# A third Winograd step for P4 in two products of a dense layer on Trainium2

## Chip, cores and metric

The kernel runs on one core of one Trainium2 chip. The metric is the device time of one execution in microseconds (us); lower is better. All data are fp32.

## What is computed

Two layers follow each other on x of 8 sequences, 256 tokens, 1024 channels. The first adds to x a dense product with W and a low-rank (LoRA) term whose experts are chosen for each token; the second adds a product with one of 16 matrices, chosen for each sequence.

```python
base = jnp.einsum('btd,od->bto', x, W)
logits = jnp.einsum('btd,ed->bte', x, Wr) + bias        # bias: 5.0 at the sequence's own expert
topw, topi = jax.lax.top_k(logits, 2)
weights = jax.nn.softmax(topw, axis=-1)
gates = jnp.sum(jax.nn.one_hot(topi, 8) * weights[..., None], axis=-2)
h = jnp.einsum('btd,erd->bter', x, A)                   # 8 experts of rank 16
x = x + base + 2.0 * jnp.einsum('bter,bte,eor->bto', h, gates, B)
x = x + jnp.einsum('bsi,boi->bso', x, L1_weight[adapter_ids])
```

Only layer one's dense product (`x + base`, and B of the LoRA term) is touched by the change.

## The kernel before, in words

**Layer one** is a matrix product in Winograd's form of Strassen's method: seven products in place of eight, and sums and differences of blocks around them. The outer step cuts W and x into 2 x 2 blocks each (`wb`, `xb`; a block of W is 512 x 512, one of x 512 channels by 1024 tokens) and makes seven products, with the keys "1" to "7" (`opening` makes key "1", `product` the others; they run in the order 1, 5, 2, 6, 3, 7, 4, lines 760 to 816). The residual is an identity added to W's diagonal blocks. Results are gathered in `yb`, four blocks of 128 x 4096, each seen as four quarters `dest[:, q]` of 128 x 1024.

**The second step** is inside each product: `make_subs` (L366) gives views `a(i, j)`, `b(i, j)` of quarters of the two factors, and their sums s1 to s3 and t1 to t3. `product` (L504) then runs seven inner products on TensorE (PE): a00 b00 into A, s1 t1 into B, s2 t2 into A, a01 b10 into X (a copy of A, made by ScalarE at L522), s3 t3 into A, **P3**, that is s2 b11, into B, and **P4**, that is a11 t2, into A. A, B and X are pairs of PSUM banks (128 x 2 x 512). Each inner product is four matmul calls (`mm`, L442 to L453): two chunks k of 128 channels, two halves m of 128 outputs, 512 tokens. The s2 and t2 that P3 and P4 read are remade by `late[0]` and `late[1]` (L562, L566). Where `lora` is given, `mm` adds the up projection, two more calls on B's rows and the gated `hg` (L443, L444).

**The third step** is in the products with `further` set (keys 5, 2, 3, 4): there a01 b10 goes down once more, as seven small products of one chunk, 128 outputs and 256 tokens (`deep`, L512). Their factors are differences r1 to r4 (128 x 128) and q1 to q4 (128 x 256), made by VectorE from `make_subs` (L390 to L403) into pool `sub3`, one buffer for each of the tags r13, r2, r4, q13, q2, q4. Two of PSUM's single banks, A3 and B3, gather what belongs to several quarters, and the rest goes into X itself. VectorE adds A3 (L551, L561, L576) and B3 (L577) into `dest[:, 0]`, and then X (L578).

**Who does what, in which order.** Each engine runs its instructions in the order in which the program issues them (`manual_schedule`, L752); the framework adds the waits. VectorE (DVE) does all sums and differences, and adds each accumulator into its quarter: `evict` (L431) is an addition on DVE where a base is given, and a copy on ScalarE where none is. All DVE additions are recorded under one line, L217. In between stands `pump(place)` (L335): it takes pieces of work off the list `todo` (block differences, the s, t, r, q of a later product, in pieces with an estimated time and an earliest place) and issues a share of what is left over the places 1 to 7. A pumped piece stands in DVE's queue ahead of what is issued after it.

In products 2 and 4 the base and the destination are y21 to y11 and y21 to y21 (L797, L816). During product 2, `todo` holds differences of x22, x12, w11 and w22 and the s and t of key 6; during product 4 it holds `prep_w1(0, 0)` and `prep_y(0)`, the adapter's first preparations.

**PSUM pairs rotate.** `roles` (L105) gives the next product the pair of the last one's X as A, that of B as X, and that of A as B. So the B of the product behind 2 (key 6, not `further`, which begins with four calls into A and then wants B) and that behind 4 (`adapt(0)`, the adapter of the first sequence, L648, likewise) stand on the pair that P4 was gathered in, and wait until DVE has read it. The single banks are also used by the transposes of `turn` and the last adapter.

**Layer two** (`adapt`, L648) is one Winograd step for each of the eight sequences, with the weights loaded by the SP queue (`load_w1`, L603) into the space of blocks that are read no more.

The end of `product`, where P3 and P4 stand:

```python
add(dest[:, 0], X, dest[:, 0])
pump(4)
mm(A, t["s3"], t["t3"])
add(dest[:, 3], A, dest[:, 3])
pump(5)
mm(B, t["s2"], b(1, 1), False, "d", 1)
add(dest[:, 1], B, dest[:, 1])
pump(6)
mm(A, a(1, 1), t["t2"], False, "1", 0)
evict(dest[:, 2], A, old[2])
pump(7)
```

Of the kernel before, what the change touches and what calls it, by code (L numbers as in the profile page):

```python
# [9 lines left out]
F32 = mybir.dt.float32  # L10
# [6 lines left out]
P = 128  # L17
# [8 lines left out]
def kernel(  # L26
# [320 lines left out]
    def us(n):  # L347
        return (n + 151) / 960
# [13 lines left out]
        return pieces(fn, wb[out_], wb[x], wb[y], 2)  # L362

    subs = {}

    def make_subs(key, w, x, further=True):  # L366

        def a(i, j):  # L370
            return wb[w][:, 2 * j : 2 * j + 2, i * OQ : (i + 1) * OQ]

        def b(i, j):
            return xb[x][:, 2 * i : 2 * i + 2, j * TQ : (j + 1) * TQ]


        ra = lambda i, j: a(0, 1)[:, j, ts(i, P)]
        rb = lambda i, j: b(1, 0)[:, i, ts(j, TQ // 2)]
        t = {}

        def op3(name, tag, fn, x, y, first=4):
            width = P if name[0] == "r" else TQ // 2

            def run():
                t[name] = sub3.tile([P, width], F32, name=f"{name}_{key}", tag=tag)
                fn(t[name], *(t[v] if isinstance(v, str) else v for v in (x, y)))

            return us(width), first, run

        deep = [  # L390
            op3("r1", "r13", add, ra(1, 0), ra(1, 1)),
            op3("q1", "q13", minus, rb(0, 1), rb(0, 0)),
            op3("r2", "r2", minus, "r1", ra(0, 0)),
            op3("q2", "q2", minus, rb(1, 1), "q1"),
            op3("r4", "r4", minus, ra(0, 1), "r2"),
            op3("q4", "q4", minus, rb(1, 0), "q2"),
        ]

        def deep3():
            for o in (  # L400
                op3("r3", "r13", minus, ra(0, 0), ra(1, 0)),
                op3("q3", "q13", minus, rb(1, 1), rb(0, 1)),
            ):  # L403
                o[2]()

        def op(name, fn, x, y, first):
            pool = sub2 if name[1] == "2" else sub1
            width = OQ if name[0] == "s" else TQ

            def run():  # L410
                t[name] = pool.tile([P, 2, width], F32, name=f"{name}_{key}", tag=name)
                fn(t[name], *(t[v] if isinstance(v, str) else v for v in (x, y)))

            return us(2 * width), first, run

        def late_s():
            minus(t["s2"], a(0, 1), t["s2"])

        def late_t():
            minus(t["t2"], b(1, 0), t["t2"])  # L420

        subs[key] = (a, b, t, (late_s, late_t), (ra, rb, deep3), further)
        return [
            op("s1", add, a(1, 0), a(1, 1), 3),
            op("t1", minus, b(0, 1), b(0, 0), 3),
            op("s2", minus, "s1", a(0, 0), 3),
            op("t2", minus, b(1, 1), "t1", 3),
            op("s3", minus, a(0, 0), a(1, 0), 5),
            op("t3", minus, b(1, 1), b(0, 1), 5),
        ] + (deep if further else [])  # L430

    def evict(dest, acc, base=None):

# [24 lines left out]
    def opening(key, dest):  # L458


        idle = pair("idle", 2)
        for i in range(WARM):
            nc.tensor.matmul(idle[:, 0, :P], lhsT=ident, rhs=ident, start=True, stop=True)  # L463
        mm = multiply()
        sums_of = make_subs(key, "11", "11", False)
        a, b, t, late, _, _ = subs.pop(key)
        X = pair(f"X_{key}", 0)
        A = pair(f"A_{key}", 1)
        add_identity(wb["11"], 0, 2)
        mm(X, a(0, 1), b(1, 0), True, part=(0,))  # L470
        project(0, 0, singles("ps_h_0_0"), (2,), last=False)
        mm(X, a(0, 1), b(1, 0), part=(1,))
        evict(dest[:, 0], X)
        project(0, 0, None, (3,), False, False)
        mm(A, a(0, 0), b(0, 0), True, part=(0,))
        project(0, 0, None, (0,), False, False)
        mm(A, a(0, 0), b(0, 0), part=(1,))
        project(0, 0, None, (1,), False, False)
        use_adapter_ids()
        add_identity(wb["11"], 2, 4)  # L480
        for s in sums_of[:4]:
            s[2]()
        add(dest[:, 0], A, dest[:, 0])
        nc.tensor.matmul(idle[:, 1, :NB], lhsT=ones, rhs=ids_f[:, :NB], start=True, stop=True)
        use_ids(idle[:, 1, :NB])
        B = pair(f"B_{key}", 2)
        mm(B, t["s1"], t["t1"], True)
        evict(dest[:, 3], B)
        for s in sums_of[4:]:
            s[2]()  # L490
        mm(A, t["s2"], t["t2"])
        evict(dest[:, 1], A)
        project(0, 0, None, range(KH, KC), False)
        take(0, 0)
        for f in late:
            f()
        mm(A, t["s3"], t["t3"])
        add(dest[:, 3], A, dest[:, 3])
        mm(B, t["s2"], b(1, 1))
        add(dest[:, 1], B, dest[:, 1])  # L500
        mm(A, a(1, 1), t["t2"])
        evict(dest[:, 2], A)

    def product(key, base, dest, lora=None, tokens=None):  # L504

        a, b, t, late, (ra, rb, deep3), further = subs.pop(key)
        mm = multiply(dict(zip("01d", b_part(lora))) if lora is not None else None, tokens)
        new = roles(key)
        old = [base[:, q] if base is not None else None for q in range(4)]
        n0, n1 = (slice(j * (TQ // 2), (j + 1) * (TQ // 2)) for j in range(2))  # L510

        def deep(acc, lhs, rhs, first=False):  # L512
            nc.tensor.matmul(acc, lhsT=lhs, rhs=rhs, start=first, stop=True, skip_group_check=True)  # L513

        def quarter(m, n):

            return dest[:, 0][:, m, n], old[0][:, m, n] if base is not None else None

        A = new("A")
        mm(A, a(0, 0), b(0, 0), True)  # L520
        X = new("X")
        nc.scalar.copy(X, A)  # L522
        if not further:
            pump(1)
            B = new("B")
            mm(B, t["s1"], t["t1"], True, "1", 1)
            evict(dest[:, 3], B, old[3])
            pump(3)
            mm(A, t["s2"], t["t2"])
            evict(dest[:, 1], A, old[1])  # L530
            pump(3)
            mm(X, a(0, 1), b(1, 0), False, "0", 0)
            late[0]()
            late[1]()
            evict(dest[:, 0], X, old[0])
# [8 lines that stand above are left out]
            evict(dest[:, 2], A, old[2])  # L544
            pump(7)
            return
        A3 = single(f"A3_{key}", 0)[:, n0]
        deep(A3, ra(0, 0), rb(0, 0), True)
        q, o = quarter(0, n0)
        evict(q, A3, o)  # L550
        pump(1)  # L551
        B = new("B")
        mm(B, t["s1"], t["t1"], True, "1", 1, ms=(0,))
        B3 = single(f"B3_{key}", 1)[:, n0]
        deep(B3, t["r1"], t["q1"], True)
        deep3()
        mm(A, t["s2"], t["t2"])
        evict(dest[:, 1], A, old[1])
        deep(A3, t["r2"], t["q2"])
        q, o = quarter(0, n1)  # L560
        evict(q, A3, o)  # L561
        late[0]()  # L562
        pump(2)
        mm(B, t["s1"], t["t1"], True, "1", 1, ms=(1,))
        evict(dest[:, 3], B, old[3])
        late[1]()  # L566
        pump(3)
        deep(X[:, 0, n0], ra(0, 1), rb(1, 0))
        deep(X[:, 0, n1], t["r4"], rb(1, 1))
        deep(X[:, 1, n0], ra(1, 1), t["q4"])  # L570
        mm(X, None, None, False, "0", 0, part=())
        deep(A3, t["r3"], t["q3"])
        two = [P, 2, TQ // 2]
        d1 = dest[:, 0][:, 1, :].rearrange("p (j n) -> p j n", j=2)
        both = A3.unsqueeze(1).to_broadcast(two)
        evict(d1, both, old[0][:, 1, :].rearrange("p (j n) -> p j n", j=2) if base is not None else None)  # L576
        add(dest[:, 0][:, :, n1], B3.unsqueeze(1).to_broadcast(two), dest[:, 0][:, :, n1])  # L577
        add(dest[:, 0], X, dest[:, 0])  # L578
        pump(4)
        mm(A, t["s3"], t["t3"])  # L580
        add(dest[:, 3], A, dest[:, 3])
        pump(5)
        mm(B, t["s2"], b(1, 1), False, "d", 1)
        add(dest[:, 1], B, dest[:, 1])
        pump(6)
        mm(A, a(1, 1), t["t2"], False, "1", 0)
        evict(dest[:, 2], A, old[2])
        pump(7)
# [285 lines left out]
```

## Time and profile before

| what | value |
|---|---|
| median of three runs | 428.77 us (428.74 to 429.66) |
| the profiled execution's own time | 430.16 us |
| its span, first to last instruction | 428.4 us |
| mean granted clock of TensorE | 0.999 |
| TensorE busy | 423.1 us (99%) |
| VectorE busy | 281.7 us (66%) |
| ScalarE busy | 39.6 us (9%) |
| DMA | 55.83 MB, 130 GB/s over the span |
| product 2 on TensorE | 92.98 to 123.47 us of the span |
| product 4 on TensorE | 202.03 to 232.52 us of the span |

All times in a view are counted from the start of the span. PE stands for TensorE's matmuls, PEld for its weight loads, DVE for VectorE. A fp32 matmul call leaves two records, each with a weight load of its own. Matmuls are pipelined, so a record is longer than the distance to the next one (592 ns against 429 for 512 columns); lengths are best read from the distance between starts. A line of the timeline gives the start, the length, engine, line, operation, output and inputs, shape, how many were merged and, in brackets, the idle time before and what ended it.

### The profile page before, as it was taken

Reading aid. Unit: us, or ns where it says so; the run is one execution under the profiler, and the core shown is the slowest. Engines: PE = TensorE matmul, PEld = TensorE weight load, DVE = VectorE, ACT = ScalarE, POOL = GpSimd, SP = SyncE. Lnnn points to the kernel's source line nnn. Section 1 sums busy time; section 2 is a strip of 40 time slices with the busy share of each in tenths; the row PEclk is TensorE's granted clock in tenths of the full one; section 3 lists DMA queues with packets and bytes.
Section 4 is the critical chain, followed back from the end, with each engine's and each line's share of the span. In section 5 each row is a group of like instructions: output and inputs, shape, how many; then the busy total and the mean of one; then the engine's idle time right before and its main releaser. Section 6 shows DMA issues by size and latency. Waiting matters only on the chain.

```text
span 428.4 us, 3335 instructions
## 1 busy us (share of the span) xinstructions
PE 423.1 (99%) x1246; PEld 217.3 (51%) x1246; DVE 281.7 (66%) x375; ACT 39.6 (9%) x65; POOL 2.0 (0%) x10
## 2 busy tenths in 40 slices
PE   8999999999999999999999999999999999999996
PEld 5566984545444445444454444444444444444574
DVE  1627288956988959889595676565756576565531
ACT  1120022110000000000000101010110101010110
POOL 1000000000000000000000000000000000000000
PEclk9999999999999999999999999999999999999999
DMA  8995000000000140630302276556748385550202
GB/s 279 383 398 217 2 0 2 0 0 2 0 0 0 31 168 0 249 142 0 99 0 98 98 262 227 199 207 208 272 148 313 128 275 214 196 197 0 98 2 99
DMA packets 14305, 55.83 MB, mean 130 GB/s; under 512 B 1232, under 2 KB 3536, under 8 KB 9808
## 3 DMA queue, kind: packets, MB, share of 16 engines
q1 hardware_dynamic: 12976, 54.68, 35.5%
q10 hardware_dynamic: 1248, 0.93, 0.7%
q8 instruction: 10, 0.16, 0.2%
q14 instruction: 7, 0.06, 0.0%
q0 software_dynamic: 64, 0.00, 0.0%
HBM read 47.22 MB, written 8.39 MB: 130 GB/s over the span
## 4 chain that ended last, share of the span: by engine, by line
PE 98%; DVE 0%; POOL 0%; issue 0%; ACT 0%; POOLq 0%; DVEq 0%
PE A L447 24%; PE A L660 22%; PE B L447 14%; PE B L660 13%; PE ps_h L245 7%; PE X L660 6%; PE X L447 4%; PE A_last L718 3%; PE A L513 1%; PE X L513 1%; PE idle L463 1%; PE ps_g L315 0%; PE B L513 0%; DVE y L217 0%; ACT z L748 0%
## 5 line engine op out<-in xcount | busy, mean ns | idle before, releaser
L660 PE MATMUL B<-x,x 128*128 128x512 f32 x128 | 57.5, 592 | 0.0
L447 PE MATMUL A<-t,s 128*128 128x512 f32 x112 | 50.3, 592 | 0.0
L217 DVE TENSOR_TENSOR y<-A,y 128x1024 f32<-128x1024 f32 (+2 forms) x27 | 26.3, 985 | 25.1 <-PE A L447 14.2
L660 PE MATMUL A<-w,x 128*128 128x512 f32 x88 | 39.6, 592 | 0.0
L660 PEld LDWEIGHTS B<-x,x 128*128 128x128 f32 x128 | 24.3, 190 | 29.8 <-issue 29.7
L217 DVE TENSOR_TENSOR w<-w,w 128x1024 f32<-128x1024 f32 x24 | 29.0, 1223 | 15.4 <-PE A L660 15.3
L660 PE MATMUL A<-w,y 128*128 128x512 f32 x88 | 39.1, 592 | 0.0
L447 PEld LDWEIGHTS A<-t,s 128*128 128x128 f32 x112 | 21.2, 190 | 22.9 <-issue 22.5
L245 PEld LDWEIGHTS ps_h<-y,x 128*128 128x128 f32 x256 | 30.7, 191 | 3.3 <-issue 3.3
L245 PE MATMUL ps_h<-y,x 128*128 128x136 f32 x256 | 30.6, 279 | 0.0
L660 PEld LDWEIGHTS A<-w,x 128*128 128x128 f32 x88 | 16.7, 190 | 21.0 <-issue 21.0
L660 PEld LDWEIGHTS A<-w,y 128*128 128x128 f32 x88 | 16.7, 190 | 21.0 <-issue 21.0
L435 ACT COPY z<-A 128x512 f32<-128x512 f32 x21 | 12.3, 586 | 158.3 <-PE A L660 158.3
L447 PE MATMUL B<-t,s 128*128 128x512 f32 x56 | 25.9, 594 | 0.3 <-DVE bias L200 0.3
L447 PE MATMUL A<-x,w 128*128 128x512 f32 x56 | 25.3, 592 | 0.0
L447 PE MATMUL A<-t,w 128*128 128x512 f32 x56 | 25.2, 592 | 0.0
L447 PE MATMUL B<-x,s 128*128 128x512 f32 x56 | 25.2, 592 | 0.0
L217 DVE TENSOR_TENSOR y<-B,y 128x1024 f32<-128x1024 f32 (+1 forms) x16 | 17.4, 1090 | 9.5 <-PE B L447 8.7
L217 DVE TENSOR_TENSOR x<-x,x 128x1024 f32<-128x1024 f32 (+1 forms) x20 | 19.2, 1004 | 0.0
L447 PEld LDWEIGHTS B<-x,s 128*128 128x128 f32 x56 | 10.6, 190 | 13.4 <-issue 12.7
L447 PEld LDWEIGHTS A<-t,w 128*128 128x128 f32 x56 | 10.6, 190 | 13.4 <-issue 12.7
L217 DVE TENSOR_TENSOR z<-X,z 128x512 f32<-128x512 f32 x8 | 5.5, 692 | 17.9 <-PE X L660 15.9
(119 smaller groups left out, 446.3 us busy)
## 6 DMA issues: line engine op xcount, KB each, us to landing
x<-w_dram SPq DMA_DIRECT2D x24, 1024.0 KB, 4.8
w<-w_dram SPq DMA_DIRECT2D x8, 1024.0 KB, 4.8
out_dram<-z SPq DMA_DIRECT2D x15, 512.0 KB, 3.0
x<-xT_dram SPq DMA_DIRECT2D x6, 1024.0 KB, 12.9
w<-wT_dram SPq DMA_DIRECT2D x3, 1024.0 KB, 14.9
x<-xT_dram SPq DMA_DIRECT2D x4, 256.0 KB, 3.8
x<-xT_dram SPq DMA_DIRECT2D x2, 512.0 KB, 7.4
w<-w11T_dram SPq DMA_DIRECT2D x1, 512.0 KB, 6.1
```

What stands on the lines that cost most here:

```text
L217: nc.vector.tensor_tensor(out_, x, y, op)
L245: nc.tensor.matmul(ps[v][:, u * EA : (u + 1) * EA], lhsT=xk(k, j, c)[:, ts(r, P)], rhs=aw_sb[:, k, :], start=(first and k == some[0] and u ...
L435: nc.scalar.copy(dest, acc)
L447: nc.tensor.matmul(acc[:, m, :], lhsT=l, rhs=r, start=(first and i < len(ms)), stop=(i >= len(steps) - len(ms)), skip_group_check=True,)
L463: nc.tensor.matmul(idle[:, 0, :P], lhsT=ident, rhs=ident, start=True, stop=True)
L513: nc.tensor.matmul(acc, lhsT=lhs, rhs=rhs, start=first, stop=True, skip_group_check=True)
L660: nc.tensor.matmul(accs[name], lhsT=lhs[:, k // 2, k % 2, :], rhs=rhs[:, k, :], start=(first and k == 0), stop=(k == KH - 1), skip_group_c ...
L718: nc.tensor.matmul(acc, lhsT=lhs[:, k // 2, k % 2, :], rhs=rhs[:, k, ts(v, m)], start=(first and k == 0), stop=(k == KH - 1), skip_group_c ...
```

## The change

In the products of keys 2 and 4, P4 is no longer four calls of 512 tokens but takes the third step down as well: seven calls of 256 tokens, with r1 to r4 made from quarters of a11 and q1 to q4 from quarters of t2. To that end the code of the third step moves from `make_subs` and `product` into a new function `third`, which gives back the first six differences (`ops`), the last two (`ops3`), the small products (`piece`) and their additions into a destination (`take`). For a01 b10, and in products 5 and 3, it issues what was issued before.

The new instructions of P4 stand so: the six differences on DVE ahead of the addition of X; piece 1 and its take behind s3 t3 and its addition; piece 5, r3 and q3, piece 6 and its take behind P3; then, past `pump(6)`, the two calls of the up projection into A, the pieces 2, 3, 4 into A, piece 7, the takes 7 and 5 into quarter 2, and the addition of A into quarter 2. P4's single banks are the two that the third step of a01 b10 used. A piece that writes P1's bank again stands behind the take that reads it.

```diff
@@ -362,6 +362,65 @@
         return pieces(fn, wb[out_], wb[x], wb[y], 2)
 
     subs = {}
+    NQ = TQ // 2
+    def third(key, lhs, rhs):
+        ra = lambda i, j: lhs()[:, j, ts(i, P)]
+        rb = lambda i, j: rhs()[:, i, ts(j, NQ)]
+        n0, n1 = slice(0, NQ), slice(NQ, TQ)
+        t, own = {}, {}
+        def op(name, tag, fn, x, y):
+            width = P if name[0] == "r" else NQ
+            def run():
+                t[name] = sub3.tile([P, width], F32, name=f"{name}_{key}", tag=tag)
+                fn(t[name], *(t[v] if isinstance(v, str) else v() for v in (x, y)))
+            return us(width), 4, run
+        A, B = (lambda i, j: lambda: ra(i, j)), (lambda i, j: lambda: rb(i, j))
+        ops = [
+            op("r1", "r13", add, A(1, 0), A(1, 1)),
+            op("q1", "q13", minus, B(0, 1), B(0, 0)),
+            op("r2", "r2", minus, "r1", A(0, 0)),
+            op("q2", "q2", minus, B(1, 1), "q1"),
+            op("r4", "r4", minus, A(0, 1), "r2"),
+            op("q4", "q4", minus, B(1, 0), "q2"),
+        ]
+        def ops3():
+            op("r3", "r13", minus, A(0, 0), A(1, 0))[2]()
+            op("q3", "q13", minus, B(1, 1), B(0, 1))[2]()
+        def piece(n, acc=None):
+            if n in (1, 5):
+                own[n] = single(f"P{n}_{key}", n // 5)[:, n0]
+            out_, l, r = {
+                1: lambda: (own[1], ra(0, 0), rb(0, 0)),
+                2: lambda: (acc[:, 0, n0], ra(0, 1), rb(1, 0)),
+                3: lambda: (acc[:, 0, n1], t["r4"], rb(1, 1)),
+                4: lambda: (acc[:, 1, n0], ra(1, 1), t["q4"]),
+                5: lambda: (own[5], t["r1"], t["q1"]),
+                6: lambda: (own[1], t["r2"], t["q2"]),
+                7: lambda: (own[1], t["r3"], t["q3"]),
+            }[n]()
+            nc.tensor.matmul(out_, lhsT=l, rhs=r, start=(n in (1, 5)), stop=True, skip_group_check=True)
+        def take(n, dest, base=None):
+            cut = lambda v: {1: v[:, 0, n0], 6: v[:, 0, n1], 5: v[:, :, n1]}[n]
+            if n == 7:
+                cut = lambda v: v[:, 1, :].rearrange("p (j n) -> p j n", j=2)
+            src = own[5 if n == 5 else 1]
+            if n in (5, 7):
+                src = src.unsqueeze(1).to_broadcast([P, 2, NQ])
+            evict(cut(dest), src, None if base is None else cut(base))
+        return ops, ops3, piece, take
 
     def make_subs(key, w, x, further=True):
 
...
+        two = key in ("2", "4")
+        _, ops3, piece, take = deep
+        piece(1)
+        take(1, dest[:, 0], old[0])
         pump(1)
         B = new("B")
         mm(B, t["s1"], t["t1"], True, "1", 1, ms=(0,))
-        B3 = single(f"B3_{key}", 1)[:, n0]
-        deep(B3, t["r1"], t["q1"], True)
-        deep3()
+        piece(5)
+        ops3()
         mm(A, t["s2"], t["t2"])
         evict(dest[:, 1], A, old[1])
-        deep(A3, t["r2"], t["q2"])
-        q, o = quarter(0, n1)
-        evict(q, A3, o)
+        piece(6)
+        take(6, dest[:, 0], old[0])
         late[0]()
         pump(2)
         mm(B, t["s1"], t["t1"], True, "1", 1, ms=(1,))
         evict(dest[:, 3], B, old[3])
         late[1]()
         pump(3)
-        deep(X[:, 0, n0], ra(0, 1), rb(1, 0))
-        deep(X[:, 0, n1], t["r4"], rb(1, 1))
-        deep(X[:, 1, n0], ra(1, 1), t["q4"])
+        for n in (2, 3, 4):
+            piece(n, X)
         mm(X, None, None, False, "0", 0, part=())
-        deep(A3, t["r3"], t["q3"])
-        two = [P, 2, TQ // 2]
-        d1 = dest[:, 0][:, 1, :].rearrange("p (j n) -> p j n", j=2)
-        both = A3.unsqueeze(1).to_broadcast(two)
-        evict(d1, both, old[0][:, 1, :].rearrange("p (j n) -> p j n", j=2) if base is not None else None)
-        add(dest[:, 0][:, :, n1], B3.unsqueeze(1).to_broadcast(two), dest[:, 0][:, :, n1])
+        piece(7)
+        take(7, dest[:, 0], old[0])
+        take(5, dest[:, 0], dest[:, 0])
+        if two:
+            ops, ops3, piece, take = third(f"{key}b", lambda: a(1, 1), lambda: t["t2"])
+            for o in ops:
+                o[2]()
         add(dest[:, 0], X, dest[:, 0])
         pump(4)
         mm(A, t["s3"], t["t3"])
         add(dest[:, 3], A, dest[:, 3])
+        if two:
+            piece(1)
+            take(1, dest[:, 2], old[2])
         pump(5)
         mm(B, t["s2"], b(1, 1), False, "d", 1)
+        if two:
+            piece(5)
+            ops3()
+            piece(6)
+            take(6, dest[:, 2], old[2])
         add(dest[:, 1], B, dest[:, 1])
         pump(6)
+        if two:
+            mm(A, None, None, False, "1", 0, part=())
+            for n in (2, 3, 4):
+                piece(n, A)
+            piece(7)
+            take(7, dest[:, 2], old[2])
+            take(5, dest[:, 2], dest[:, 2])
+            add(dest[:, 2], A, dest[:, 2])
+            pump(7)
+            return
         mm(A, a(1, 1), t["t2"], False, "1", 0)
         evict(dest[:, 2], A, old[2])
         pump(7)
```

More of the change, by code (lines that the diff above doesn't have):

```diff
@@ L374, in b @@
             return xb[x][:, 2 * i : 2 * i + 2, j * TQ : (j + 1) * TQ]
-        ra = lambda i, j: a(0, 1)[:, j, ts(i, P)]
-        rb = lambda i, j: b(1, 0)[:, i, ts(j, TQ // 2)]
         t = {}
[L381 to L404, printed above, removed]
         def op(name, fn, x, y, first):
@@ L420, in late_t @@
             minus(t["t2"], b(1, 0), t["t2"])
-        subs[key] = (a, b, t, (late_s, late_t), (ra, rb, deep3), further)
+        deep = third(key, lambda: a(0, 1), lambda: b(1, 0)) if further else None
+        subs[key] = (a, b, t, (late_s, late_t), deep)
         return [
@@ L429, in make_subs @@
             op("t3", minus, b(1, 1), b(0, 1), 5),
-        ] + (deep if further else [])
+        ] + (deep[0] if further else [])
     def evict(dest, acc, base=None):
@@ L465, in opening @@
         sums_of = make_subs(key, "11", "11", False)
-        a, b, t, late, _, _ = subs.pop(key)
+        a, b, t, late, _ = subs.pop(key)
         X = pair(f"X_{key}", 0)
@@ L504, in product @@
     def product(key, base, dest, lora=None, tokens=None):
-        a, b, t, late, (ra, rb, deep3), further = subs.pop(key)
+        a, b, t, late, deep = subs.pop(key)
         mm = multiply(dict(zip("01d", b_part(lora))) if lora is not None else None, tokens)
@@ L509, in product @@
         old = [base[:, q] if base is not None else None for q in range(4)]
[L510 to L517, printed above, removed]
         A = new("A")
@@ L522, in product @@
         nc.scalar.copy(X, A)
-        if not further:
+        if deep is None:
             pump(1)
@@ L546, in product @@
             return
-        A3 = single(f"A3_{key}", 0)[:, n0]
-        deep(A3, ra(0, 0), rb(0, 0), True)
-        q, o = quarter(0, n0)
-        evict(q, A3, o)
+        two = key in ("2", "4")
+        _, ops3, piece, take = deep
+        piece(1)
+        take(1, dest[:, 0], old[0])
         pump(1)
@@ L553, in product @@
         mm(B, t["s1"], t["t1"], True, "1", 1, ms=(0,))
-        B3 = single(f"B3_{key}", 1)[:, n0]
-        deep(B3, t["r1"], t["q1"], True)
-        deep3()
+        piece(5)
+        ops3()
         mm(A, t["s2"], t["t2"])
         evict(dest[:, 1], A, old[1])
-        deep(A3, t["r2"], t["q2"])
-        q, o = quarter(0, n1)
-        evict(q, A3, o)
+        piece(6)
+        take(6, dest[:, 0], old[0])
         late[0]()
```

## The prediction

> **What bounds the kernel now.** I read the page first: the busy shares, and the chain that ended last.
>
> ```profile
> PE 423.1 (99%) x1246; PEld 217.3 (51%) x1246; DVE 281.7 (66%) x375; ACT 39.6 (9%) x65; POOL 2.0 (0%) x10
> PE 98%; DVE 0%; POOL 0%; issue 0%; ACT 0%; POOLq 0%; DVEq 0%
> ```
>
> TensorE (PE) is the bound over the whole span, and its clock is full in every slice. Less work on PE is worth its full length, unless PE then waits. Next I read the chain in order of time (start us, us, what), around the product of key 2:
>
> ```profile
> 106.30 1.29 PE X L513 x6
> ...
> 113.17 5.15 PE B L447 x12
> 118.32 8.58 PE A L447 x20
> 126.91 3.43 PE B L447 x8
> ```
>
> Each matmul call leaves two records. Six records with 256 columns take 1.29 us, so one such call takes 0.43; eight records with 512 columns take 3.43, so one such call takes 0.858. A call of half the width costs half, whatever stands beside it. The 20 records at 118.32 are P4 (four calls and two LoRA calls, 5.15) and the first part of product 6 (3.43).
>
> Then the timeline of VectorE (DVE), at the end of product 2:
>
> ```profile
> 110.00 2.36 DVE L217 TENSOR_TENSOR w<-w,w 128x1024 f32<-128x1024 f32 x2
> 112.28 0.69 DVE L217 TENSOR_TENSOR y<-A,y 128x512 f32<-128x512 f32 x1
> 113.00 0.69 DVE L217 TENSOR_TENSOR y<-B,y 128x512 f32<-128x512 f32 x1
> 113.73 1.23 DVE L217 TENSOR_TENSOR y<-X,y 128x1024 f32<-128x1024 f32 x1
> ...
> 116.60 1.22 DVE L217 TENSOR_TENSOR y<-A,y 128x1024 f32<-128x1024 f32 x1
> 117.73 0.68 DVE L217 TENSOR_TENSOR s<-s,w 128x512 f32<-128x512 f32 x1
> 118.33 1.22 DVE L217 TENSOR_TENSOR t<-x,t 128x1024 f32<-128x1024 f32 x1
> 119.47 1.22 DVE L217 TENSOR_TENSOR y<-B,y 128x1024 f32<-128x1024 f32 x1
> ...
> 123.51 1.23 DVE L217 TENSOR_TENSOR y<-A,y 128x1024 f32<-128x1024 f32 x1 [1.09 <-PE A L447]
> ```
>
> From 107.7 to 122.3 DVE has no gap at all. At 116.60 it adds an A that PE had finished at 113.2: DVE is 3.4 us behind. Starts give the pace of independent work: 1.13 us for 1024 elements, 0.60 for 512, 0.335 for 256, 0.205 for 128 (the last two from the six r and q instructions at 89.87 to 91.48). One that reads what the one before wrote starts after its end: 112.28 to 113.00 is 0.72. The same backlog shows in PE's weight loads, the one place where PE already feels it; beside it is the only restart of PE after a DVE wait:
>
> ```profile
> 117.31 0.19 PEld L447 LDWEIGHTS B<-hg,bdiff 128*128 128x128 f32 x1 [0.24 <-issue]
> 117.87 0.48 PEld L447 LDWEIGHTS A<-t,w 128*128 128x128 f32 x2 [0.38 <-DVE y L217]
> ```
>
> ```profile
> 17.37 3.70 PE L447 MATMUL B<-t,s 128*128 128x512 f32 x8 [0.32 <-DVE bias L200]
> 20.90 0.59 PE L447 MATMUL A<-t,s 128*128 128x512 f32 x1
> ```
>
> P4's first weight load, due at 117.74, waited for the add to end at 117.82 and started 0.05 later; the matmul was still on time, since a load runs some 0.4 ahead. After a real stop, the eight records from 17.37 took 3.53 to the next start instead of 3.43, so a restart costs 0.05 + 0.10 = 0.15 after DVE's end (I keep 0.05 and 0.25 as bounds). Product 4 has the same code but an emptier DVE:
>
> ```profile
> 219.05 0.69 DVE L217 TENSOR_TENSOR y<-A,y 128x512 f32<-128x512 f32 x1
> ...
> 222.77 1.22 DVE L217 TENSOR_TENSOR y<-A,y 128x1024 f32<-128x1024 f32 x1
> 223.90 1.22 DVE L217 TENSOR_TENSOR w<-x 128x1024 f32<-128x1024 f32 x1
> 227.41 1.23 DVE L217 TENSOR_TENSOR y<-B,y 128x1024 f32<-128x1024 f32 x1 [2.29 <-PE B L447]
> ...
> 232.56 1.23 DVE L217 TENSOR_TENSOR y<-A,y 128x1024 f32<-128x1024 f32 x1 [2.60 <-PE A L447]
> ```
>
> There DVE idles 2.29 and 2.60 us before its adds.
>
> **What the Trainium skill says.** "VectorE: DVE Perf Modes", section on the TRN2 errata: an fp32 tensor_tensor of N elements takes (N+151)/0.96 ns, a fixed part per instruction. That is 424 ns for 256 and 1224 for 1024; the trace has 422 and 1223. Small pieces are dear, then. "TensorE: Matmul & The Clock Gate", section Back-to-back issue gap: a matmul's pace is proportional to its columns plus 2.5 ns. The trace agrees within a few ns (0.2146 us a record of 256, 0.429 of 512). "Perfetto Trace Analysis", section Per-engine timelines: DVE is strict FIFO, PE may pull weight loads ahead. The load at 117.87 shows the limit of that: it stood behind a DVE wait.
>
> **The change, part by part.**
>
> *PE work.* Per product, four calls of 512 columns (4 x 0.858 = 3.43) become seven of 256 (7 x 0.43 = 3.01). Saved 0.43, twice 0.86. The two LoRA calls stay.
>
> *DVE work.* Added ahead of the add of X: r1, q1, r2, q2, r4, q4, 3 x 0.205 + 3 x 0.335 = 1.62. Then take 1 (0.335), r3 and q3 (0.54), take 6 (0.335), takes 7 and 5 (0.72 each, since what follows reads the result of each). The last add stays (1.13). Sum 4.27 us per product. DMA, ScalarE, POOL and SP lose and gain nothing, and the weight loads issued behind product 4 overwrite x21, whose last readers are not moved.
>
> *New waits.* Piece 6 overwrites P1's bank, so it waits for take 1, which stands in DVE's queue behind the add of A. Everything on PE is queued behind piece 6. Piece 7 waits for take 6. Pair A, which the next product takes as its B, is free only after takes 7 and 5 and the add; until now one add stood there.
>
> *Product 2 in times.* PE (starts of records): piece 1 at 113.01 (it needs the earlier take 7, that of the product into X, to end at 112.97, a slip of up to 0.2 that the next wait swallows), B at 113.44, piece 5 at 118.59, piece 6 due at 119.02. DVE: take 5 at 113.00, r1 at 113.61, q4 done with at 115.22; X to 116.36, s and t to 118.09, add of A to 119.22, take 1 from 119.22 to its end at 119.65. Piece 6 starts at 119.65 + 0.15 = 119.80, **a wait of 0.78**. LoRA 1.72, pieces 2, 3, 4 1.29: piece 7 at 123.24; product 6 starts at 123.67, its B is due 3.43 later at 127.10. DVE goes on: s, t to 121.29; r3, q3 to 121.83; take 6 to 122.17 (ends 122.25, early for piece 7); add of B to 123.30; s, t to 125.03; take 7 at 125.03, take 5 at 125.75, add at 126.47, ending at 127.70. B of product 6 starts at 127.85, **a second wait of 0.75**. Before it started at 126.75, so product 2 **loses 1.10** (0.78 + 0.75 - 0.43). Later in product 6 DVE's work is 1.1 late as PE's is; it has 0.54 and 0.46 gaps left before its adds, and A and B come free over 2 us ahead of need, so nothing more is lost there.
>
> *Product 4 in times.* DVE: take 5 at 219.77, the six to 222.00, X to 223.13, w to 224.27, add of A to 225.40, take 1 ends 225.82. Piece 6 is due at 228.07: no wait. r3 waits for piece 5's end (228.24); take 6 from 228.82 ends 229.24; piece 7 at 231.50 does not wait. The stage ends at 231.93 instead of 232.35. Takes 7 and 5 from 232.14, add from 233.58 to 234.82; with 0.15 B is free at 234.97, and adapt(0) wants it at 231.93 + 3.43 = 235.36. **0.39 to spare**, and 0.43 gained. DVE's following work comes 1.0 later, but before it had 1.35 and 0.49 us of idle time ahead of the next weight differences.
>
> **Sum.** +1.10 - 0.43 = +0.67 us. The profiled execution would go from 430.16 to 430.83 (span 428.4 to 429.1). The median of the runs is 1.4 lower than the profiled time, and the change is added to it: 428.77 + 0.67 = 429.44.
>
> **Rivals.**
> *Hidden:* DVE's work costs PE nothing. For it: DVE is 66% busy. Against it: no gap from 107.7 to 122.3. 428.77 - 0.86 = 427.91. Chance 0.08.
> *Half hidden:* piece 6 waits, the handing over of pair A doesn't. Product 2 then costs 0.78 - 0.43 = +0.35, product 4 -0.43: 428.69. Against it: the takes have a backlog of s and t before them. Chance 0.10.
> *Slower:* the handing over of pair A fails after product 4 too. For it: three dependent instructions (2.68 us) under a cover of 3.43. It decides once DVE is over 0.83 late there (0.39 to spare, and 0.44 of idle time from 231.70 to 232.14). If take 7 starts 1.2 after piece 7's end, as worked out for product 2 (125.03 against 123.83), PE waits 1.16 - 0.39 = 0.77 more: 430.21. Against it: the idle times in product 4. Chance 0.22.
>
> **How the numbers follow.** My forecast, 429.44, has 0.60; its own range is 429.1 to 429.8 (restarts of 0.05 to 0.25 twice, and some 0.15 for the runs). Measurement tells about 0.2%, 0.86 us, from no change, so the bounds lie at 427.91 and 429.63. Of the forecast's chance 0.14 lies above 429.63; with 0.22 that is 0.36 slower. Hidden lies on its bound: 0.05 faster. The rest, 0.59, is within. The range, 428.5 to 430.3, holds forecast, half hidden and slower; it leaves out hidden and the tails.
>
> **What would show it.** In product 2, a weight load that waits for DVE ahead of the second r,q piece of P4 by about 0.8 us, and one ahead of product 6's B of about 0.7; take 1 in DVE's queue right behind the add of A, near 119.2. In product 4 neither, and the adapter stage 0.4 earlier against its product. The forecast is wrong if PE goes through product 2 without idle time, or if adapt(0)'s B waits.

## The result and the profile after

| | before | changed |
|---|---|---|
| median of ten runs each, side by side on one chip | 429.11 us | 430.29 us |
| lowest and highest | 428.74, 429.66 | 429.42, 430.67 |
| profiled execution, own time | 430.16 us | 430.37 us |
| its span | 428.4 us | 428.6 us |

The changed kernel takes 1.0025 of the time of before, 95% interval 1.0015 to 1.0035: 1.07 us more, between 0.64 and 1.50. (The ratio is that of the means; the medians are 1.18 apart.) The prediction had +0.67, which lies just inside that interval. The 428.77 that it started from, the median of three runs, lies 0.34 below the median of the ten, so its 429.44 is to be read as a difference. The 0.25% is just above the bound of 0.2% named there; its interval reaches below it.

The two profiled spans differ by only 0.2 us. This is the first thing to clear up, and a table of landmarks does it: starts of matmuls in the timeline of PE, counted from the start of the span.

| landmark | before | changed |
|---|---|---|
| first inner product into B of the opening (key 1) | 17.37 | 16.86 |
| first matmul of product 2 | 92.82 | 92.31 |
| first into B of product 6 | 126.75 | 127.33 |
| s3 t3 of product 4 | 218.62 | 219.28 |
| first matmul of the adapter | 232.35 | 232.60 |
| product 2 to B of product 6 | 33.93 | 35.02 |
| product 2 to s3 t3 of product 4 | 125.80 | 126.97 |
| from there to the adapter | 13.73 | 13.32 |
| product 2 to the adapter | 139.53 | 140.29 |

Most of the lines behind the table, in before and then in the changed kernel:

```profile
92.82 3.60 PE L447 MATMUL A<-x,w 128*128 128x512 f32 x8
126.75 3.60 PE L447 MATMUL B<-t,s 128*128 128x512 f32 x8
218.62 3.60 PE L447 MATMUL A<-t,s 128*128 128x512 f32 x8
232.35 3.60 PE L660 MATMUL A<-w,y 128*128 128x512 f32 x8
```

```profile
92.31 3.60 PE L479 MATMUL A<-x,w 128*128 128x512 f32 x8
219.28 3.60 PE L479 MATMUL A<-t,s 128*128 128x512 f32 x8
232.60 3.60 PE L699 MATMUL A<-w,y 128*128 128x512 f32 x8
236.04 3.60 PE L699 MATMUL B<-x,x 128*128 128x512 f32 x8
```

The opening was 0.51 shorter in the changed kernel's execution, ahead of anything that the change touches. From the first product into B to product 2 it is 75.45 us in both, and from the adapter's first matmul to the end of the span 196.0 in both. So distances between landmarks compare the kernels, and ends of spans do not. By them product 2 and what follows at once loses 1.09, a further 0.08 is lost by s3 t3 of product 4, and product 4 gains 0.41: +0.76.

The page, its busy row and the shares of the chain:

```profile
PE 422.0 (98%) x1258; PEld 219.2 (51%) x1258; DVE 289.5 (68%) x399; ACT 39.6 (9%) x65; POOL 2.0 (0%) x10
PE 90%; DVE 6%; DMA 3%; issue 0%; ACTq 0%; ACT 0%; DVEq 0%
```

PE has less to do and the kernel is longer. VectorE (DVE) now holds 6% of the chain where it had 0%. These 6% are not the loss: they are 24.3 us in one row, DVE's queue without a gap from 102.89, where DVE had last waited for PE, to 127.19. (The 3% of DMA lie in the opening, ahead of the change.) The chain in order of time (start us, us, what) shows the row's two ends:

```profile
102.89 1.56 DVE y L217 x2
...
124.60 0.61 DVE y L217
...
125.23 0.70 DVE y L217
...
125.96 1.24 DVE y L217
127.19 0.14 issue
127.33 3.67 PE B L479 x8
...
232.77 3.43 PE A L699 x8
236.20 3.43 PE B L699 x8
```

Ahead of product 6's B stand takes 7 and 5 and the addition of A, one after the other. Ahead of the adapter's B (236.20) stands PE alone: the same handing over costs nothing there. DVE waits for piece 7 in product 4 and is done at 235.47, ahead of the 236.04 at which B is due:

```profile
232.81 1.42 DVE L217 TENSOR_TENSOR y<-P_4b,y 128x512 f32<-128x512 f32 x2 [0.46 <-PE P_4b L411]
234.25 1.22 DVE L217 TENSOR_TENSOR y<-A,y 128x1024 f32<-128x1024 f32 x1
```

The timeline of DVE and the weight loads in product 2:

```profile
117.57 1.22 DVE L217 TENSOR_TENSOR y<-A,y 128x1024 f32<-128x1024 f32 x1
118.71 0.42 DVE L217 TENSOR_TENSOR y<-P_2b,y 128x256 f32<-128x256 f32 x1
...
124.51 1.42 DVE L217 TENSOR_TENSOR y<-P_2b,y 128x512 f32<-128x512 f32 x2
125.96 1.22 DVE L217 TENSOR_TENSOR y<-A,y 128x1024 f32<-128x1024 f32 x1
```

```profile
118.20 0.19 PEld L411 LDWEIGHTS P_2b<-q_2b,r_2b 128*128 128x128 f32 x1 [0.24 <-issue]
119.18 0.30 PEld L411 LDWEIGHTS P_2b<-q_2b,r_2b 128*128 128x128 f32 x2 [0.79 <-DVE y L217]
...
127.30 0.30 PEld L479 LDWEIGHTS B<-t,s 128*128 128x128 f32 x2 [1.37 <-PE A L479]
```

Take 1 (118.71) ends at 119.13, and piece 6's weight load follows at 119.18. The last addition ends at 127.18, and the load of product 6's B follows at 127.30. Its line names PE's A as what it waited for, the chain and the matmul's own line name DVE; the experiment that moves the sums of place 6 decides for DVE. In the timeline of PE piece 6's matmul and B of product 6 are the only two, after the opening, with idle time before them:

```profile
119.18 0.70 PE L411 MATMUL P_2b<-q_2b,r_2b 128*128 128x256 f32 x2 [0.39 <-DVE y L217]
...
123.16 3.60 PE L479 MATMUL A<-x,w 128*128 128x512 f32 x8
127.33 3.67 PE L479 MATMUL B<-t,s 128*128 128x512 f32 x8 [0.57 <-DVE y L217]
```

The idle times 0.39 and 0.57 are not the loss. A record is longer than the distance to the next one, so the tail of the matmul before hides part of it. By starts, B was due at 123.16 + 3.43 = 126.59 and came at 127.33, 0.74 late. Piece 6 was due at 118.63 and came 0.55 late, with 0.10 lost behind it in the restart (the next call follows after 0.53 in place of 0.43). (By a restart the first matmuls behind a stop of PE are meant.)

### The profile page after: what moved, and what is told of

Read it like the earlier page. It is cut to its first block, busy times and chain, and to the rows that moved or that the text cites. A ratio compares the mean times of both kernels' runs of the same rounds, so it can differ in the third digit from the quotient of the medians.

```text
span 428.6 us, 3384 instructions
## 1 busy us (share of the span) xinstructions
PE 422.0 (98%) x1258; PEld 219.2 (51%) x1258; DVE 289.5 (68%) x399; ACT 39.6 (9%) x65; POOL 2.0 (0%) x10
## 4 chain that ended last, share of the span: by engine, by line
PE 90%; DVE 6%; DMA 3%; issue 0%; ACTq 0%; ACT 0%; DVEq 0%
PE A L699 22%; PE A L479 20%; PE B L699 13%; PE B L479 13%; PE X L699 6%; PE ps_h L245 6%; PE A_last L757 3%; PE X L479 3%; DVE y L217 3%; DMA x<-xT_dram 2%; DVE t L217 1%; PE P L411 1%; DMA y<-awT_dram 1%; PE X L411 1%; DVE s L217 1%; DVE x L217 1%
## 5 line engine op out<-in xcount | busy, mean ns | idle before, releaser
L699 PEld LDWEIGHTS B<-x,x 128*128 128x128 f32 x128 | 24.3, 190 | 29.7 <-issue 29.6
L217 DVE TENSOR_TENSOR y<-A,y 128x1024 f32<-128x1024 f32 x18 | 22.0, 1223 | 12.2 <-PE A L479 12.1
L217 DVE TENSOR_TENSOR y<-B,y 128x1024 f32<-128x1024 f32 x12 | 14.7, 1222 | 5.7 <-PE B L479 5.7
L479 PE MATMUL A<-t,w 128*128 128x512 f32 x40 | 18.0, 592 | 0.0
L217 DVE TENSOR_TENSOR t<-x 128x1024 f32<-128x1024 f32 x14 | 17.1, 1220 | 0.5 <-DMA x<-xT_dram 0.5
L217 DVE TENSOR_TENSOR t<-x,t 128x1024 f32<-128x1024 f32 x14 | 17.1, 1219 | 0.0
```

The source lines that it names most:

```text
L217: nc.vector.tensor_tensor(out_, x, y, op)
L479: nc.tensor.matmul(acc[:, m, :], lhsT=l, rhs=r, start=(first and i < len(ms)), stop=(i >= len(steps) - len(ms)), skip_group_check=True,)
L699: nc.tensor.matmul(accs[name], lhsT=lhs[:, k // 2, k % 2, :], rhs=rhs[:, k, :], start=(first and k == 0), stop=(k == KH - 1), skip_group_c ...
```

## Experiments

All ratios are against the kernel before, on the same chip, with 95% intervals; "distance" is product 2 to the adapter, 139.53 in before. The edits are to the changed kernel except where another is named. My theory was that the loss is made by two waits of PE for DVE in product 2, and that product 4 has its full gain. The rivals were an equal loss in each product, waits that each cost their own length, and a cost of the small matmuls.

**Product 4 alone, product 2 alone.**

```diff
-        two = key in ("2", "4")
+        two = key == "4"        # the first run
+        two = key == "2"        # the second run
```

> P4 takes the third step in product 4 alone; product 2 is as before the change. My theory (the loss is two waits of PE for VectorE in product 2, and product 4 gains its full 0.43 us): 0.43 us faster than before, 0.999 of its time, no PE wait for VectorE between product 4 and the first adapter. Rival (the small pieces and their differences cost something in each product, half the measured loss each): 0.5 us slower than before.

> P4 takes the third step in product 2 alone. My theory: 1.1 us slower than before (waits of 0.78 ahead of piece 6 and 0.7 ahead of the next product's B, less 0.43), so 1.0026 of its time, and 0.4 slower than the changed kernel. Rival (an equal cost in each product): 0.5 us slower than before.

Measured: 0.9989 (0.9983 to 0.9996) for product 4 alone, distance 139.12, that is 0.41 less; 1.0026 (1.0016 to 1.0036) for product 2 alone, distance 140.70, that is 1.17 more. The equal loss is out: product 4 gains, product 2 loses, and the two add up to the changed kernel's +0.76. These two runs also show that moving the old code into `third` costs nothing: where P4 is left as four calls, product 2 to B of product 6 is 33.92 (33.93 in before), and product 4's s3 t3 to the adapter 13.73 as in before.

**VectorE's part without the small matmuls.** In the kernel before's form of P4, with the six differences made and read by nobody:

```diff
-        two = key in ("2", "4")
+        two = False
...
+        if key == "2":
+            for o in third("2b", lambda: a(1, 1), lambda: t["t2"])[0]:
+                o[2]()
         add(dest[:, 0], X, dest[:, 0])
```

> The kernel before, with P4 as four calls in both products; only the first six differences r and q of the third step of P4 are made in product 2, where the changed kernel makes them, and nothing reads them. My theory (VectorE's queue, not the small matmuls, makes the loss): 1.62 us more ahead of the addition of A, of which 0.13 goes into a dependency that no longer waits, so P4's first weight load waits until 119.36 in the times of before instead of 117.87, its matmul starts 1.3 late, and the kernel is 1.3 us slower than before, more than the whole change. Rival (the loss comes from small matmuls and from restarting accumulation): no slower than before.

Measured: 1.0030 (1.0019 to 1.0041), distance 140.83, 1.30 more. The weight loads ahead of P4:

```profile
116.09 0.19 PEld L479 LDWEIGHTS B<-hg,bdiff 128*128 128x128 f32 x1 [0.24 <-issue]
118.14 0.30 PEld L479 LDWEIGHTS A<-t,w 128*128 128x128 f32 x2 [1.86 <-DVE y L217]
```

In before the same load waited 0.38, of which 0.24 is the usual distance; here it is 1.86. Six instructions of 0.28 to 0.42 us on an engine that is busy 66% of the span cost PE 1.3 us, since at this place the addition of A was already the last thing that PE waited for. No small matmul is needed for a loss of this size.

**Each wait by itself.** The pumped sums of place 4 (s1 and t1 of product 6) moved behind take 1:

```diff
-        pump(4)
+        if key != "2":
+            pump(4)
         mm(A, t["s3"], t["t3"])
...
             take(1, dest[:, 2], old[2])
+        if key == "2":
+            pump(4)
         pump(5)
```

> The changed kernel, but in product 2 the pumped sums of place 4 (s and t, 1.73 us) stand behind take 1 instead of ahead of the addition of A. My theory: the wait ahead of piece 6 is gone, but VectorE has the same work ahead of the last addition, which ends at the same time, so the next product's B starts when it did: 1.5 us of wait there in place of 0.78 and 0.75, and the same time as the changed kernel (1.0 to 1.1 us slower than before). Rival (each wait costs its own length): 0.78 us faster than the changed kernel.

Measured: 1.0020 (1.0012 to 1.0027), distance 140.29, the changed kernel's to the hundredth. The timeline of PE:

```profile
118.53 1.03 PE L411 MATMUL P_2b<-q_2b,r_2b 128*128 128x256 f32 x4
...
127.67 0.67 PE L479 MATMUL B<-t,s 128*128 128x512 f32 x1 [1.23 <-DVE y L217]
```

Pieces 5 and 6 now stand in one row, without a wait. All that was saved there is waited for at B: idle 1.23 in place of 0.57. Both waits come from the same backlog of DVE, and its length up to the last addition sets when B can start, whether PE has waited before or not.

The sums of place 6 (s3 and t3 of product 6) moved behind the last addition:

```diff
         add(dest[:, 1], B, dest[:, 1])
-        pump(6)
+        if key != "2":
+            pump(6)
...
             add(dest[:, 2], A, dest[:, 2])
+            if key == "2":
+                pump(6)
             pump(7)
```

> The changed kernel, but in product 2 the pumped sums of place 6 (s and t, 1.73 us) stand behind the last addition of A. My theory: the wait of 0.78 ahead of piece 6 stays, the one ahead of the next product's B goes, since VectorE now waits for piece 7 and ends 2.7 us behind it, under 3.43 us of PE work: 0.75 us faster than the changed kernel, and within 0.1 of before. Rival (the three dependent additions cannot be covered even so): no faster than the changed kernel.

Measured: 0.9998 (0.9990 to 1.0006), distance 139.48: 0.81 less than the changed kernel. DVE's timeline shows why:

```profile
122.05 1.22 DVE L217 TENSOR_TENSOR y<-B,y 128x1024 f32<-128x1024 f32 x1
123.77 1.42 DVE L217 TENSOR_TENSOR y<-P_2b,y 128x512 f32<-128x512 f32 x2 [0.50 <-PE P_2b L411]
125.22 1.23 DVE L217 TENSOR_TENSOR y<-A,y 128x1024 f32<-128x1024 f32 x1
```

DVE is now the one that waits (0.50, for piece 7). The three dependent additions take 2.7 us from there (123.77 to 126.45) and end before product 6's B is due at 127.00. The wait ahead of piece 6 is still there.

**Both moves, and product 3 with them.** The two edits together; then also with keys 2, 3, 4 in `two` and both moves for keys 2 and 3.

> The changed kernel with both moves in product 2: the pumped sums of place 4 behind take 1, those of place 6 behind the last addition. My theory: both waits of PE go, since VectorE's 1.73 us of place 6 leave the stretch that sets the hand-over; A is free at 126.1 in the times of before, when the next product's B is due at 126.3; 0.86 us faster than before, 0.998 of its time, and the next product takes the late sums without a wait. Rival (VectorE is full over both products, so the work moved is missed later, in the next product): at best 0.4 us faster than before, with a PE wait in the next product.

> As the run with both moves, and P4 of product 3 takes the third step too, with the same two moves there. My theory: product 3 has more room on VectorE (idle 1.35 and 2.11 us before two additions), take 1 ends near 170.5 where piece 6 is due at 173.5, and pair A is free near 180.4 where B is due at 180.8 in the times of before: another 0.43 us, 1.29 us faster than before, 0.997 of its time. Rival (its hand-over fails as product 2's did): no faster than with two products.

Measured: 0.9988 (0.9980 to 0.9997), distance 138.82, 0.71 less; and 0.9973 (0.9965 to 0.9980), distance 138.41, 1.12 less. Neither has a PE wait for DVE at piece 6 or at a B behind a product. In the first of the two, pieces 5 and 6 stand in one row and B follows product 6's A after 3.43:

```profile
118.50 1.03 PE L411 MATMUL P_2b<-q_2b,r_2b 128*128 128x256 f32 x4
...
122.81 3.60 PE L479 MATMUL A<-x,w 128*128 128x512 f32 x8
126.24 3.60 PE L479 MATMUL B<-t,s 128*128 128x512 f32 x8
```

The weight loads that still show DVE lose nothing, except one. That one (here in the same run) is the difference between 0.71 and the 0.86 expected, for the most part:

```profile
111.95 0.19 PEld L479 LDWEIGHTS A<-t,s 128*128 128x128 f32 x1 [0.24 <-issue]
112.81 0.30 PEld L411 LDWEIGHTS P_2b<-t,w 128*128 128x128 f32 x2 [0.67 <-DVE y L217]
```

Piece 1 takes the bank of the earlier product's P1, and waits for take 7 of that; it costs 0.11 (product 2 to B of product 6 is 33.62, 0.31 less than before and not 0.43). In the changed kernel the wait at piece 6 swallows it. Product 4 gives 0.41, product 3 another 0.41. Whether product 3 needs the moves was not run. The run with three products is the fastest of all kernels here, 428.18 us beside 429.52. That DVE is too full over both products was not borne out: product 6 takes the late sums without a PE wait.

**The moves in the kernel before.** The same two moves, P4 as four calls.

> The kernel before with the two moves of pumped sums in product 2 and nothing else. My theory: PE waited for nothing there, so the moves alone give nothing: within 0.1 us of before. Rival (the order of the sums was a cost already): up to 0.8 us faster than before.

Measured: 0.9997 (0.9988 to 1.0006), distance 139.53, as before to the hundredth. The moves are worth nothing by themselves; they only let the third step have its gain.

## Why the prediction was right

- *PE work, 0.43 a product.* Right: 0.41 measured in product 4 and, with the moves, in product 3, where nothing waits.
- *DVE's work, 4.27 us, and its order.* Right. Take 1 ends at 119.13 against 119.65 worked out, 0.51 of it being the shorter opening.
- *The first wait.* Right, place and size: 0.55 at piece 6, 0.10 in its restart and 0.11 at piece 1, 0.76 against 0.78. The slip at piece 1 was put at up to 0.2.
- *The second wait.* Right: 0.74 against 0.75, and 0.08 for the restart behind it, which I had counted into the start of B. So 0.08 more is lost than the 1.10 forecast: 1.17 by s3 t3 of product 4.
- *Product 4 without a wait, 0.39 to spare at the handing over.* Right: the adapter's B starts 3.44 after its A (232.60 to 236.04), and with the 0.15 of a restart behind DVE's end at 235.47 there are 0.42 to spare. The rival that the hand-over fails there too did not happen.
- *Nothing more lost in product 6, with idle times of 0.54 and 0.46 left there.* That PE loses no more is right, the reading behind it is not. DVE is not 1.1 late there: counted from the start of product 2, its last addition ends 2.95 later than before (127.18 against 124.74, with 0.51 of shorter opening). In before DVE idled 1.10 and then 0.54 in product 6; in the changed kernel both are gone, and the 0.46 stands. A is free 1.9 us ahead of its next use there (135.76 against 137.70), in before as well, and not over 2.
- *The signs.* The weight load ahead of piece 6 shows 0.79, as forecast (about 0.8); but 0.24 of it is the usual distance, and the forecast's 0.78 counted the slip and the restart, so the figures meet in part by chance. The load ahead of product 6's B shows 1.37 and not 0.7: a load runs some 0.4 ahead of its matmul, and its usual distance is in it too.
- *The time.* +0.67 forecast, +0.76 by distances in the trace, +1.07 (0.64 to 1.50) by runs. I put 0.59 on a difference within 0.2% and 0.36 on slower; the measured 0.25% falls on the other side of that bound, by less than its own uncertainty. The trace's +0.76 is 0.18%. The 0.3 between trace and runs is within the spread of the runs: in all nine comparisons with before, the difference of the distances lies inside the interval of the runs, and the run with take 1 moved, of the same distance, measured +0.20% (0.12% to 0.27%). That the median of 430.29 stands inside the stated range, which ends at 430.3, is luck: the ten runs of before lie 0.34 above the start of the forecast.

The two waits are not two prices to be added freely, which the prediction did not say: taking only the first away gained nothing, taking only the second gained 0.81, and taking the first away as well gained another 0.66 (139.48 to 138.82).

## What to carry to other kernels

Where one engine is the bound and another feeds it in a fixed order, the helper's share of busy time says little, as the 66% of DVE did here: look at how far its queue is behind at the place of the change, and at what the bound engine takes from it next. Shorter work on the bound engine brings dependent work on the helper with it; give it room by moving what is not due behind the step that hands a buffer over, and look at the last hand-over first, since an earlier wait that is removed is only paid there, as long as the helper's queue has no gap up to it. The same edit gained 0.41 us where the queue had room and lost 1.17 where it had none.

## What the hardware showed beyond that

The spread between the traced executions sits in the opening. In ten profiled executions of ten kernels the first product into B began between 16.01 and 17.37 us, and from there to product 2 it was 75.45 to 75.46 us in all of them; from the adapter's first matmul to the end of the span it was 195.96 to 196.05, where the span is given to 0.1. So a difference of 0.1 us between landmarks behind the opening can be read from one trace each, while ten runs of the kernel before lie between 428.74 and 429.66.

Behind a DVE wait, PE's weight load started 0.05 us (piece 6), 0.06 (P4 in the run without the small matmuls) and 0.12 (B of product 6) after DVE's end, and the first matmuls then lost another 0.08 to 0.11, with 256 as with 512 columns.
